# Seven block products in the order 1, 2, 5, 6, 3, 7, 4, with the fifth's copy ahead of the first quarter's rotation on ScalarE

## The chip, the cores and the metric

The kernel runs on one core of a Trainium2 chip. Its engines work beside each other, each through its own queue in order: TensorE (PE for matmuls, PEld for its weight loads), VectorE (DVE), ScalarE (ACT), GpSimd (POOL) and SyncE (SP, which issues most DMAs). The metric is the device time of one execution in microseconds (us), as the median of several runs.

## The reference

The input `x` is 32 sequences of 64 tokens with 512 values each (2048 tokens in all), the context has the same shape. Four residual layers follow each other, all in float32:

```python
x = x + L0_xattn(layernorm(x), ctx)   # 32 query heads, 8 key/value heads of 128, rotary q and k, masked softmax
x = x + L0_ffn(layernorm(x))          # silu(gate) * up, 1376 wide, weights dequantized from 4 bits
x = x + L1_xattn(layernorm(x), ctx)   # the same sizes, q and k normalized by RMS in place of the rotation
x = x + L1_ffn(layernorm(x))          # a memory of 128 slots, top 8, softmax, a gate
```

In an attention layer q = x wq, k = ctx wk, v = ctx wv; scores of the 64 queries of a sequence against its 64 keys, softmax, the weighted sum of v, and that times wo. In the first attention q and k are rotated: `q * cos + rot(q) * sin`, where `rot` exchanges the two halves of a head's 128 rows.

## The kernel before

**Tiles and stages.** The tokens are four chunks of 512 (`NCH`), and an attention layer walks over 32 steps, one for each of eight groups of four heads (`g`) and each chunk (`c`). A step projects k and v (`pk`, L356; `pv`, L388), projects q (tiles `P`, L189), computes scores (`S`, L489), softmax, the values (`po`, L590) and the product with wo (tiles `O`, L189), whose parts are added to x on VectorE (`join`, L237). The work is staggered: in one step, `Attention.run` (L653) emits the rest of the wo products of the step before, then k and q of the next step, then the values of this step, the next step's v, the first wo products, and the next step's scores. The FFN walks over six groups of columns and the four chunks, with up products (tiles `P`, weights `wgu`) and down products (tiles `D`).

**Seven products in place of eight.** The large products (q, wo, up, down) are 512x512 and cut in 2x2 blocks of 256. Each is computed with seven block products of sums of blocks (Strassen's scheme, in Winograd's form). `left_sums` and `right_sums` (L163, L171) make the sums of blocks ahead of time; `PRODUCTS` (L161) says which left and right block each of the seven takes. One block product (`product`, L181) is four float32 matmuls of 128x128 by 128x256; in the trace each shows as two records, so a product is eight records and a call of seven products 56.

**`quarters` (L199)**, which the change edits, is called by `project_q` (L449) and by the FFN's `ffn_up` (L927): 64 calls in the attentions, 24 in the FFN (the last four with half the matmuls). It emits seven products into four PSUM tiles and gives out the four quarters of the result, each as a sum of one copy `h` and one PSUM tile:

- product 1 into tile x; copy 1 of x to `h` on ScalarE (L213); product 2 into a tile of its own: quarter (0,0) is copy 1 plus product 2;
- product 6 added to x; copy 2 of x; product 5 into tile w; copy 5 of w;
- product 3 added to w: quarter (0,1) is copy 2 plus w;
- product 7 added to x; copy 3 of x: quarter (1,1) is copy 5 plus x;
- product 4: quarter (1,0) is copy 3 plus product 4.

So product 6 waits for copy 1, product 7 for copy 2 and product 3 for copy 5: each overwrites by accumulation what the copy reads.

**What `done` does with a quarter.** In the first attention, `quarter` in `project_q` adds on VectorE (L420), then `rotate` (L398) makes two copies of 64 rows on ScalarE (`rq`, L403), two products with cos and sin on VectorE (L405, L406) and a sum on GpSimd into `qT` (L407). In the second attention it is a sum (L438), a square on ScalarE (L440) and a reduction on VectorE (L444). In the FFN it is a sum (L917), silu on ScalarE (L921) for the gate half or a product on GpSimd (L924) for the up half.

**What sets the order.** A scheduler orders each engine's instructions from the order of the program and its own estimates; `tc.issue_after(ins)` adds an edge that queues the block's instructions which run on the engine of `ins` behind it. It adds no wait between engines. In the program that it builds for the kernel before, PE runs products 1, 2, 6, 5, then the first half of 7, then 3, the second half of 7, and 4; ScalarE's queue in the first attention is copy 1, the `rq` pair of the first quarter, copy 2, copy 5, the pair of the second quarter, copy 3, the pairs of the third and fourth.

**Around it.** PSUM holds six tiles of this kind (`mm_tile`, L59), shared by `pk`, `pv`, `P`, `po`, `O`, `D` and the transposes of normalized x (L270). The copies `h` share four buffers (`half_tile`, L68). During the first attention's middle groups the FFN's constants are prepared in pieces on VectorE behind the last `join` of a step (`ffn_constants`, L737, lines L754 to L815); its last group normalizes x for the FFN (`xnb`, L265; `xnT` copies on ScalarE, L274).

Of the kernel before, what the change touches and what calls it, by code (L numbers as in the profile page):

```python
# [44 lines left out]
def tile_xattn_ffn_2_layers(ctx: ExitStack, tc: tile.TileContext, a: dict, out: bass.AP):  # L45
    nc = tc.nc
# [12 lines left out]
    def mm_tile(name):  # L59
        return psp.tile([P, CH], F32, tag="mm", name=name)  # L60
# [7 lines left out]
    def half_tile(name):  # L68
        return ap_.tile([P, CH], F32, tag="half", name=name, bufs=4)
# [111 lines left out]
    def product(which, ps, left, right, widths=(P, P), first=True):  # L181


        nonlocal last_matmul
        l, r = PRODUCTS[which]
        pv = ps.rearrange("p (m n) -> p m n", m=2)
        for m, w in enumerate(widths):
            for k in range(left.shape[2]):
                ins = nc.tensor.matmul(  # L189
                    pv[0:w, m, :],  # L190
                    left[:, l, k, m * P : m * P + w],
                    right[:, r, k, :],
                    start=(first and m == 0 and k == 0),
                    stop=(k == left.shape[2] - 1),
                    skip_group_check=True,
                )
        last_matmul = ins.ins

    def quarters(n, left, right, done, widths=(P, P)):  # L199


        size = (slice(0, widths[0]), slice(0, len(widths) * HC))

        def mul(which, ps=None):
            new = ps is None
            if new:
                ps = mm_tile(f"P{which}_{n}")
            product(which, ps, left, right, widths, first=new)
            return ps

        def copy(which, ps):
            t = half_tile(f"h{which}_{n}")
            nc.scalar.copy(t[size], ps[size])  # L213
            return t

        x = mul(1)
        p1 = copy(1, x)
        done(0, 0, p1, mul(2))
        mul(6, x)
        u2 = copy(2, x)  # L220
        w = mul(5)
        p5 = copy(5, w)
        mul(3, w)
        done(0, 1, u2, w)
        mul(7, x)
        u3 = copy(3, x)
        done(1, 1, p5, x)
        done(1, 0, u3, mul(4))
# [74 lines left out]
    class Attention:  # L303
# [105 lines left out]
        def project_q(self, g, c):  # L409
# [21 lines left out]
            else:  # L431
# [3 lines left out]
                def quarter(i, f, x, y):  # L435
# [11 lines left out]
                    )  # L447

            quarters(n, self.wq[g], xnT[c], quarter)  # L449
            return qT, part  # L450

# [452 lines left out]
    def ffn_up(i, c):  # L904

        if len(ffn_tiles(i)) == 2:
            hT = ctx_tile(f"hT{i}_{c}").rearrange("p a b -> p (a b)")[:, 0 : NBLK * HC]
        else:
            hT = tmp_tile(f"hT{i}_{c}").rearrange("p a b -> p (a b)")
        hT = hT.rearrange("p (b k w) -> p b k w", k=1, w=HC)  # L910
        widths = [w_ for _, w_ in ffn_tiles(i)]
        size = (slice(0, widths[0]), slice(0, len(widths) * HC))

        def quarter(j, half, x, y):

            x, y = x[size], y[size]
            nc.vector.tensor_tensor(x, x, y, ALU.add)  # L917
            h = hT[0 : widths[0], 2 * half : 2 * half + len(widths), 0, :]
            xv = x.rearrange("p (t w) -> p t w", w=HC)
            if j == 0:  # L920
                nc.scalar.activation(xv, xv, AF.Silu)  # L921
                held[half] = xv
            else:
                nc.gpsimd.tensor_tensor(h, held[half], xv, ALU.mult)  # L924

        held = {}
        quarters(f"{i}_{c}", wgu[i], xnT[c], quarter, widths)  # L927
        if len(widths) == 2:
            left_sums(hT)
        return hT  # L930
# [452 lines left out]
```

## Time and profile before

| what | before |
|---|---|
| median of 3 runs | 2912.19 us (2910.71 to 2914.42) |
| the profiled execution | 2913.03 us, of which the span of the profile is 2911.2 |
| TensorE busy | 2824.0 us |
| VectorE, GpSimd, ScalarE busy | 1874.6, 1364.5, 820.0 us |
| q products (tiles `P`, weights `wq`), both attentions | 799.4 us busy, 3584 records |
| up products (tiles `P`, weights `wgu`) | 275.5 us busy, 1232 records |
| copies `h` on ScalarE | 200.3 us, 352 of them |
| `rq` copies on ScalarE | 157.9 us, 256 of them, 617 ns each |
| mean granted TensorE clock | 0.989 |

How to read it: the first attention lies at about 0 to 1210 us, the FFN to 1640, the second attention to about 2870, the last layer's rest behind it. A row of a timeline gives start, duration, engine, line, the operation with output and input tiles and a count, and in brackets the engine's idle time before it with what ended it. A wait row gives total idle time, how often, and the longest. Matmul records overlap: each lasts 379 ns, but the next begins 215 or 216 ns later, so a gap is read from the starts.

### The profile page before, as it was taken

Reading aid. Unit: us, or ns where it says so; the run is one execution under the profiler, and the core shown is the slowest. Engines: PE = TensorE matmul, PEld = TensorE weight load, DVE = VectorE, ACT = ScalarE, POOL = GpSimd, SP = SyncE. Lnnn points to the kernel's source line nnn. Section 1 sums busy time; section 2 is a strip of 40 time slices with the busy share of each in tenths; the row PEclk is TensorE's granted clock in tenths of the full one; section 3 lists DMA queues with packets and bytes.
Section 4 is the critical chain, followed back from the end, with each engine's and each line's share of the span. In section 5 each row is a group of like instructions: output and inputs, shape, how many; then the busy total and the mean of one; then the engine's idle time right before and its main releaser. Section 6 shows DMA issues by size and latency. Waiting matters only on the chain.

```text
span 2911.2 us, 41247 instructions
## 1 busy us (share of the span) xinstructions
PE 2824.0 (97%) x16742; PEld 2262.3 (78%) x16742; DVE 1874.6 (64%) x2809; ACT 820.0 (28%) x1397; POOL 1364.5 (47%) x1038
## 2 busy tenths in 40 slices
PE   7999999999999999899999999999999999999987
PEld 5878787778877887688888677888888888888765
DVE  7677777777777777655555655555555555555567
ACT  3333332333333333111111222222222222222233
POOL 5554545454646454544334444444444444444433
PEclk9999999999999999899999999999999999999998
DMA  4111111111111110100000101111111020201001
GB/s 162 41 41 45 52 46 51 43 52 45 55 53 56 51 45 15 37 22 15 22 14 32 50 30 58 44 51 44 55 40 61 34 66 30 66 30 66 15 1 58
DMA packets 103813, 130.77 MB, mean 45 GB/s; under 512 B 8726, under 2 KB 65166, under 8 KB 103624
## 3 DMA queue, kind: packets, MB, share of 16 engines
q1 hardware_dynamic: 103047, 127.09, 13.2%
q8 instruction: 133, 2.18, 0.3%
q10 hardware_dynamic: 576, 1.05, 0.1%
q14 instruction: 57, 0.46, 0.0%
HBM read 123.92 MB, written 4.19 MB: 44 GB/s over the span
## 4 chain that ended last, share of the span: by engine, by line
PE 85%; DVE 9%; issue 2%; ACT 2%; POOL 1%; DMA 1%; SPq 0%; DVEq 0%; ACTq 0%; POOLq 0%
PE P L189 32%; PE O L189 24%; PE pv L388 8%; PE pk L356 6%; PE po L590 4%; PE S L489 4%; PE D L189 3%; DVE x L237 2%; ACT rq L403 1%; DVE S L512 1%; DVE r2x L549 1%; PE pqy L1077 1%; PE pu L1077 1%; DVE xnd L265 0%; DMA wgu<-in_qweight_gu 0%
## 5 line engine op out<-in xcount | busy, mean ns | idle before, releaser
L189 PE MATMUL P<-xnT,wq 128*128 128x256 f32 x3584 | 799.4, 382 | 22.0 <-ACT h L213 21.7
L189 PE MATMUL O<-wo,oT 128*128 128x256 f32 x3584 | 802.1, 381 | 3.8 <-ACT oT L598 2.4
L189 PEld LDWEIGHTS P<-xnT,wq 128*128 128x128 f32 x3584 | 678.9, 191 | 157.9 <-issue 38.8
L189 PEld LDWEIGHTS O<-wo,oT 128*128 128x128 f32 x3584 | 670.3, 190 | 117.0 <-issue 25.0
L237 DVE TENSOR_TENSOR x<-x,O 128x512 f32<-128x512 f32 (+1 forms) x448 | 368.6, 823 | 228.4 <-PE O L189 228.3
L570 POOL TENSOR_TENSOR s<-s,ib 128x512 f32<-128x512 f32 x128 | 169.4, 1344 | 487.7 <-DVE ib L294 470.5
L407 POOL TENSOR_TENSOR qT<-h,rq 128x512 f32<-128x512 f32 x128 | 175.0, 1367 | 275.7 <-DVE rq L406 266.2
L213 ACT COPY h<-P 128x512 f32<-128x512 f32 (+1 forms) x352 | 200.3, 573 | 354.5 <-PE P L189 351.4
L242 POOL TENSOR_TENSOR qr<-qs,nhalf 128x20 f32<-128x20 f32 x32 | 113.3, 3542 | 358.8 <-DVE qs L477 358.4
L189 PE MATMUL P<-xnT,wgu 128*128 128x256 f32 (+1 forms) x1232 | 275.5, 384 | 2.9 <-DVE x L237 2.7
L564 ACT ACTIVATE s<-s 128x1024 f32<-128x1024 f32 x64 | 67.7, 1057 | 721.6 <-DVE s L562 721.6
L189 PEld LDWEIGHTS P<-xnT,wgu 128*128 128x128 f32 (+1 forms) x1232 | 229.2, 188 | 50.9 <-DVE x L237 11.0
L388 PE MATMUL pv<-wkv,ctxT 128*128 128x128 f32 x1984 | 246.2, 280 | 3.0 <-DVE h L420 1.7
L388 PEld LDWEIGHTS pv<-wkv,ctxT 128*128 128x128 f32 x1984 | 228.5, 192 | 24.3 <-issue 9.9
L403 ACT COPY rq<-h 64x512 f32<-64x512 f32 x256 | 157.9, 617 | 244.5 <-DVE h L420 242.2
L356 PE MATMUL pk<-ctxT,wkv 128*128 128x512 f32 x496 | 223.1, 592 | 0.0
L438 DVE TENSOR_TENSOR qT<-h,P 128x512 f32<-128x512 f32 x128 | 83.9, 674 | 163.8 <-PE P L189 163.8
L356 PEld LDWEIGHTS pk<-ctxT,wkv 128*128 128x128 f32 x496 | 94.1, 190 | 92.9 <-issue 89.6
L405 DVE TENSOR_TENSOR h<-h,cosT 128x512 f32<-128x512 f32 x128 | 90.4, 706 | 104.9 <-ACT rq L403 104.9
L917 DVE TENSOR_TENSOR h<-h,P 128x512 f32<-128x512 f32 (+1 forms) x96 | 59.6, 640 | 141.9 <-PE P L189 112.4
L924 POOL TENSOR_TENSOR hT<-h,h 128x512 f32<-128x512 f32 (+1 forms) x48 | 56.5, 1180 | 200.4 <-DVE h L917 182.7
L598 ACT COPY oT<-po 128x512 f32<-128x512 f32 x256 | 131.5, 601 | 17.7 <-PE po L590 17.0
(248 smaller groups left out, 3433.3 us busy)
## 6 DMA issues: line engine op xcount, KB each, us to landing
ctxT<-in_ctxT SPq DMA_DIRECT2D x62, 1024.0 KB
wq<-in_L_wq SPq DMA_DIRECT2D x32, 256.0 KB
wo<-in_L_wo SPq DMA_DIRECT2D x32, 256.0 KB
wq<-in_L_wqT SPq DMA_DIRECT2D x32, 256.0 KB
wo<-in_L_woT SPq DMA_DIRECT2D x32, 256.0 KB
wgu<-in_qweight_gu SPq DMA_DIRECT2D x40, 128.0 KB
out<-o SPq DMA_DIRECT2D x16, 256.0 KB
x<-in_x SPq DMA_DIRECT2D x12, 256.0 KB
```

What stands on the lines that cost most here:

```text
L189: ins = nc.tensor.matmul(pv[0:w, m, :], left[:, l, k, m * P : m * P + w], right[:, r, k, :], start=(first and m == 0 and k == 0), stop=(k ...
L213: nc.scalar.copy(t[size], ps[size])
L237: return nc.vector.tensor_tensor(dst, dst, src, ALU.add).ins
L242: return nc.gpsimd.tensor_tensor(dst, src, nhalf[:, : src.shape[-1]], ALU.pow).ins
L356: nc.tensor.matmul(ps, wkv[:, k, 0, :], ctxT[:, k, :], start=(k == 0), stop=(k == KT - 1))
L388: nc.tensor.matmul(ps[:, t * HD : (t + 1) * HD], ctxT[:, k, t * P : (t + 1) * P], wkv[:, k, 1, :], start=(k == 0), stop=(k == KT - 1),)
L403: nc.scalar.copy(t[lo:hi, 1], src[HD - hi : HD - lo])
L407: nc.gpsimd.tensor_tensor(dst(None), dst(x), dst(t[:, 1]), ALU.add)
L489: nc.tensor.matmul(s5[j * KB : (j + 1) * KB, f, e], kT[:, f, e, j], qT[:, f * 4 + j].rearrange("p h q -> p (h q)"), start=True, stop=True,)
L570: nc.gpsimd.tensor_tensor(sv[:, f], sv[:, f], ib[:, f * W : (f + 1) * W].unsqueeze(1).to_broadcast([P, KH, W]), ALU.mult,)
L590: nc.tensor.matmul(po[j][:, f * W : (f + 1) * W], v[rows, f, e], probs[rows, f, e], start=(e == 0), stop=(e == KH - 1),)
L598: ins = nc.scalar.copy(o5[:, j], po[j].rearrange("p (x q) -> p x q", q=S))
```

## The change

Inside `quarters`, product 5 and its copy are emitted ahead of products 6, and the first quarter (0,0) is given out behind copy 5, inside `tc.issue_after(last_copy)`, so that the `rq` pair (or the square, or silu) of that quarter is queued on ScalarE behind copy 5. Copy 2 then follows the pair. The seven products, the copies and the sums are the same.

```diff
         def copy(which, ps):
             t = half_tile(f"h{which}_{n}")
-            nc.scalar.copy(t[size], ps[size])
+            nonlocal last_copy
+            last_copy = nc.scalar.copy(t[size], ps[size]).ins
             return t
 
+
+        last_copy = None
         x = mul(1)
         p1 = copy(1, x)
-        done(0, 0, p1, mul(2))
+        y = mul(2)
+        w = mul(5)
+        p5 = copy(5, w)
+        with tc.issue_after(last_copy):
+            done(0, 0, p1, y)
         mul(6, x)
         u2 = copy(2, x)
-        w = mul(5)
-        p5 = copy(5, w)
         mul(3, w)
         done(0, 1, u2, w)
         mul(7, x)
```

Lines below it move down by five: the copies `h` are at L214, the sums L425, the `rq` copies L408, the later lines 5 higher than before.

## Prediction

> **What bounds the kernel now.** I read the page first: which engine is busy, at which clock, and what the chain is made of.
>
> ```profile
> PE 2824.0 (97%) x16742; PEld 2262.3 (78%) x16742; DVE 1874.6 (64%) x2809; ACT 820.0 (28%) x1397; POOL 1364.5 (47%) x1038
> ...
> PEclk9999999999999999899999999999999999999998
> ...
> PE 85%; DVE 9%; issue 2%; ACT 2%; POOL 1%; DMA 1%; SPq 0%; DVEq 0%; ACTq 0%; POOLq 0%
> ```
>
> TensorE is the bound nearly everywhere, so a change pays only by the TensorE gaps that it closes. Second, the waits of PE and of its weight loads (total us, times, longest):
>
> ```profile
> PE P L189 <- ACT h L213: 21.7, 14, 3.8
> ```
>
> ```profile
> PEld P L189 <- ACT h L213: 36.3, 69, 4.2
> ```
>
> The P products wait for ScalarE's copies `h`: 14 open gaps, and 69 late weight loads, most of them hidden. Third, the timeline of one attention call with a gap, then of one without:
>
> ```profile
> 600.80 7.07 PE L189 MATMUL P<-xnT,wq 128*128 128x256 f32 x32
> ...
> 602.73 0.59 ACT L213 COPY h<-P 128x512 f32<-128x512 f32 x1 [0.50 <-PE P L189]
> 602.90 1.88 DVE L793 CAST szoh<-zi 4x344 bf16<-4x344 uint32 x1
> ...
> 606.01 0.68 DVE L420 TENSOR_TENSOR h<-h,P 128x512 f32<-128x512 f32 x1
> ...
> 606.78 1.25 ACT L403 COPY rq<-h 64x512 f32<-64x512 f32 x2 [3.47 <-DVE h L420]
> 608.05 1.07 ACT L213 COPY h<-P 128x512 f32<-128x512 f32 x2
> ...
> 608.78 5.42 PE L189 MATMUL P<-xnT,wq 128*128 128x256 f32 x24 [0.91 <-ACT h L213]
> ```
>
> ```profile
> 708.24 12.33 PE L189 MATMUL P<-xnT,wq 128*128 128x256 f32 x56
> ...
> 712.75 1.24 ACT L403 COPY rq<-h 64x512 f32<-64x512 f32 x2 [1.99 <-DVE h L420]
> 714.01 0.58 ACT L213 COPY h<-P 128x512 f32<-128x512 f32 x1
> ...
> 715.35 0.59 ACT L213 COPY h<-P 128x512 f32<-128x512 f32 x1 [0.75 <-PE P L189]
> ...
> 715.99 4.18 PEld L189 LDWEIGHTS P<-xnT,wq 128*128 128x128 f32 x20 [0.21 <-ACT h L213]
> ```
>
> A call is 56 records, eight per product, 215.5 ns apart: 1.72 us per product. At 600.80, 32 records (products 1, 2, 6, 5) run; then product 7 (its first half stands ahead of 3) waits for copy 2, which stands behind the rotation's two `rq` copies, which wait for VectorE's sum L420, held up by the FFN's constants (L793). At 708.24 the sum is on time; there only the weight load for product 3 waits, 0.21 us, for copy 5, and the matmul starts show a step of 295 ns in place of 216.
>
> So I took from the trace's start times, call by call, the length from first to last record beyond 55 steps (11.865 us). First attention: 33.8 us in 32 calls. FFN: 6.0 in 24. Second attention: 9.1 in 32.
>
> **The change, part by part.** Times are from a call's first matmul.
>
> *Product 5 third, copy 5 second.* The built order (each engine's instructions as the scheduler leaves them) has it so in every call: PE runs 1, 2, 5, 6, 3, 7, 4 and no longer splits product 7 around 3, so that the change does what it says is settled. Copy 1 starts at 1.93 (710.17 in the second call), so copy 5, 3.45 later in PE's order, runs 5.38 to 5.96. Its readers: product 3 starts at 6.90 (32 steps), 0.9 late enough. Product 6 needs copy 1 alone. Product 5 needs its PSUM bank 1.72 earlier; in the rows of before the bank's last reader ends 2.6 us or more before it (2.6 in one short FFN call, where the move is 0.86; 3.6 elsewhere). Cost 0; without that cover at most 1.72 a call.
>
> *The rotation behind copy 5.* This is the added wait: on ScalarE the `rq` pair, copy 2, the second pair and copy 3 queue behind copy 5. The pair, which began at 4.51, begins at 5.99; with 1.25 for it and 0.61 for copy 2 (606.78 to 608.64), copy 2 ends at 7.85. Product 7 now starts after 40 steps, at 8.62, and a copy needs 0.14 to release it (608.64 to 608.78): spare 0.63. Hence product 7 stalls only where the pair starts after 6.62, that is where L420 ends after 6.53. The call at 600.80 (L420 ends at 5.9) loses its whole stall. No instruction or DMA is added but 49 semaphore instructions of 17 ns on an idle ScalarE; SP's order is unchanged.
>
> *Downstream.* The next rows have little spare: O's product 1 begins a median 0.37 us after its oT copy, pv 0.41 after L420's last. But the second quarter's sum, which ran at 9.85 (718.09), now needs product 3 at 8.8 and copy 2, so it runs at 8.9; pairs two to four and the oT copies follow 0.9 earlier. So the spare grows, and what PE gains it keeps.
>
> Sum, first attention (excess over 11.865):
> - 11 calls stalled by 0.3 to 1.4 us: 6.9, and 14 with only late weight loads: 1.6. All go: 8.5.
> - Calls at 194.70, 343.36, 488.80: 5.6 + 2.1 + 4.8 = 12.5. The pair started there at 8.82, 6.95, 7.99, so 2.20, 0.33, 1.37 stay, with 0.1 of late loads each: gain 8.2.
> - Calls at 1099.63 and 1140.00: 2.1 + 3.0. In the built order the `xnT` copies now stand behind the third and fourth pair, and a po product needs their PSUM bank: by the same chaining the second xnT copy ends at 17.1 instead of 15.9, and pv starts where it did. Gain 0.3.
> - Start: the call at 39.89 keeps its stall (ScalarE's exp still stands ahead of copy 2), but VectorE's built order puts the last sums ahead of two normalisations, for which pv waited 1.7 (63.35). I take 1.0; bounds -0.5 and 1.7.
>
> FFN: 20 calls lose 0.106 each, 2.2 (the rest is VectorE's joins). Second attention: 9.1 less 6.0 of the call at 1668.50, where exp stands ahead of the late copy before and after: 3.1.
>
> 8.5 + 8.2 + 0.3 + 1.0 + 2.2 + 3.1 = 23.3 us. The profiled execution took 2913.03 (span 2911.2, 1.8 around it), the median of three is 2912.19: 2889.7 and 2888.9. I say **2889**.
>
> Of the 8.2, 3.1 is clock: after the stalls of 3.82 and 2.99 us about eight matmuls ran at twice the step; none did after 2.88 or 2.01.
>
> ```profile
> 206.00:208.00 2.00, 2.00 (x7) 0.58 0.00 0
> ```
>
> The column 0.58 is the granted clock just after the first. The stalls left over (2.20, 1.37) are below both, so I take it all back. The Trainium skill ("TensorE: Matmul & The Clock Gate", "Part 1: The HAM clock gate") puts the return to half clock after an idle window of about 3.4 us; the trace agrees for 3.82 and differs for 2.99. By that rule alone the second call's 1.7 us would not hang on its stall, and the sum would be 21.6.
>
> **The rivals.**
> - *Late loads only move.* Product 7 has 0.63 spare, but loads were late at spares of up to 0.07 in the rows; if 0.63 does not cover them either, 1.6 + 2.2 + 3.1 are not gained: 2896. Against: calls with 0.44 to 0.6 spare at record 32 (708.24 is one) show no step there.
> - *Given back at O and pv.* If the later rows keep their place in time (the rotation is bound by VectorE and POOL, not by PE), each first-attention call keeps at most 0.37: 14 small ones 1.6, 14 others 5.0, and 5.3 from the other stages: 2901. Against: in the call at 708.24 each later pair waits for a sum that waits for PE (718.09, idle 2.78 for PE).
> - *Not slower, but the same:* VectorE's sum was the cause and is not moved; if it slips by as much as the slack gained (its order with POOL changes): 2910.
> - *Slower: product 7 becomes the stall.* The pair begins 1.5 us later everywhere. If the sum L420 were held with it (it is not in the built order, where only ScalarE's instructions follow copy 5), or the pair and copy 2 took 0.63 longer, all 32 first-attention calls stall. It decides at a copy 2 ending at 8.48; at 9.6, 1.1 us a call, 35 us are lost against 23 gained: 2924. The Trainium skill (same page, the table of specifications) calls ScalarE's queue strictly first in, first out, so the pair can't pass a late copy 5; the trace agrees (608.05: two copies back to back behind the pair).
>
> **How the numbers follow.** Forecast 0.62 (alone 2884 to 2894); late loads 0.12; given back 0.14; the same 0.07; slower 0.05. The range leaves out the last two: from the full recovery of the left-over stalls (2881) to given back (2902). A measurement tells 0.2% (5.8 us) from no change, so faster is the first three less a bit, 0.86; same 0.08; slower 0.06.
>
> **What would show it.** Right: PE's waits of P for h fall from 21.7 to about 10, in six or seven places; PEld's from 36.3 to under 15; most attention calls take 56 records in 12.2 us without a gap; O's wait for oT does not grow; the `rq` pair begins 6.0 after a call's start. Wrong: a gap at record 40 in the calls without VectorE's extra work, a larger "O <- oT" or "pv <- h", or steps of 295 ns at records 33 or 41.

## The result, and the profile after

The changed kernel takes 2894.39 us in the median of six runs (2890.91 to 2897.4), the kernel before on the same chip 2913.8 (2910.71 to 2917.59): a ratio of 0.9931, with a 95% interval of 0.9921 to 0.9941. The profiled execution took 2894.59 us, 18.4 less than that of before; 23.3 were forecast (2889, range 2881 to 2902).

The page of the changed kernel, engines and chain:

```profile
PE 2816.7 (97%) x16742; PEld 2270.3 (78%) x16742; DVE 1892.6 (65%) x2809; ACT 824.6 (29%) x1397; POOL 1345.6 (47%) x1038
...
PE 88%; DVE 6%; POOL 1%; ACT 1%; issue 1%; DMA 1%; SPq 0%; DVEq 0%; ACTq 0%; POOLq 0%
```

VectorE has gone from 9% to 6% of the chain, ScalarE from 2% to 1%. The waits of PE (total us, times, longest), then that of its weight loads:

```profile
PE P L189 <- ACT h L214: 9.7, 5, 3.8
...
PE po L595 <- ACT xnT L279: 2.5, 2, 1.3
PE O L189 <- ACT oT L603: 2.4, 2, 1.2
...
PE pv L393 <- DVE h L425: 1.6, 4, 0.6
```

```profile
PEld P L189 <- ACT h L214: 11.1, 7, 4.2
```

The wait for `h` fell from 21.7 to 9.7 and from 36.3 to 11.1 for the loads; O's wait for oT is what it was. The wait of po for `xnT`, 2.5 us, is new (before, pv waited 1.3 us for it). The call that stood at 600.80 with a gap of 0.91 us:

```profile
590.82 12.25 PE L189 MATMUL P<-xnT,wq 128*128 128x256 f32 x56
...
596.20 0.58 ACT L214 COPY h<-P 128x512 f32<-128x512 f32 x1 [2.87 <-PE P L189]
596.52 0.68 DVE L425 TENSOR_TENSOR h<-h,P 128x512 f32<-128x512 f32 x1
...
597.29 1.24 ACT L408 COPY rq<-h 64x512 f32<-64x512 f32 x2 [0.51 <-DVE h L425]
598.56 0.58 ACT L214 COPY h<-P 128x512 f32<-128x512 f32 x1
```

The sum ends 6.4 us into the call, later than before (5.9), and the pair follows it. But copy 5 is already done (596.20 to 596.78), copy 2 ends at 599.14, 8.3 us into the call, and product 7 is due only at 8.6: all 56 records run without a step longer than 216 ns. This holds for 24 of the 32 first-attention calls, now 11.87 us long.

The time by stage, from the start times of the calls' first matmuls (us; the excess is call length beyond 11.865, summed):

| stretch | before | changed | gain |
|---|---|---|---|
| to the third call | 86.56 | 87.90 | -1.3 |
| third call to the last but one | 1013.07 | 999.78 | 13.3 |
| from there to the FFN's first call | 114.46 | 115.34 | -0.9 |
| FFN | 429.46 | 424.69 | 4.8 |
| second attention to its last call | 1137.06 | 1132.37 | 4.7 |
| the rest of the span | 130.58 | 132.72 | -2.1 |
| excess, first attention | 33.8 | 13.5 | 20.4 |

The last row is the important one: the q calls of the first attention alone became 20.4 us shorter, yet the first attention (the first three rows) only 11.1.

### The profile page after: what moved, and what is told of

Read it like the earlier page. It is cut to its first block, busy times and chain, and to the rows that moved or that the text cites. A ratio compares the mean times of both kernels' runs of the same rounds, so it can differ in the third digit from the quotient of the medians.

```text
span 2892.8 us, 41295 instructions
## 1 busy us (share of the span) xinstructions
PE 2816.7 (97%) x16742; PEld 2270.3 (78%) x16742; DVE 1892.6 (65%) x2809; ACT 824.6 (29%) x1397; POOL 1345.6 (47%) x1038
## 4 chain that ended last, share of the span: by engine, by line
PE 88%; DVE 6%; POOL 1%; ACT 1%; issue 1%; DMA 1%; SPq 0%; DVEq 0%; ACTq 0%; POOLq 0%
PE P L189 33%; PE O L189 26%; PE pv L393 8%; PE pk L361 7%; PE S L494 4%; PE po L595 4%; PE D L189 3%; DVE x L242 1%; ACT rq L408 1%; PE pqy L1082 1%; PE pu L1082 1%; DVE h L425 0%; DVE h L410 0%; PE pd L962 0%; DVE xnd L270 0%
## 5 line engine op out<-in xcount | busy, mean ns | idle before, releaser
L189 PE MATMUL P<-xnT,wq 128*128 128x256 f32 x3584 | 787.8, 380 | 10.0 <-ACT h L214 9.7
L214 ACT COPY h<-P 128x512 f32<-128x512 f32 (+1 forms) x352 | 202.4, 575 | 567.5 <-PE P L189 557.0
L408 ACT COPY rq<-h 64x512 f32<-64x512 f32 x256 | 157.9, 617 | 124.8 <-DVE h L425 119.8
L449 DVE TRANSPOSE_TENSOR_REDUCE part<-q 128x16 f32<-128x512 f32 x128 | 90.6, 709 | 91.6 <-ACT q L445 87.7
```

Source lines behind the costliest of these rows:

```text
L189: ins = nc.tensor.matmul(pv[0:w, m, :], left[:, l, k, m * P : m * P + w], right[:, r, k, :], start=(first and m == 0 and k == 0), stop=(k ...
L214: last_copy = nc.scalar.copy(t[size], ps[size]).ins
L408: nc.scalar.copy(t[lo:hi, 1], src[HD - hi : HD - lo])
```

## The experiments

**Theory:** what pays is that copy 5 is queued ahead of the rotation pair *and* that product 7 comes a product later, so that the copy behind the pair is wanted 1.72 us later. **Rivals:** the product order alone, or the place in the queue alone, gives the gain; VectorE's lateness is not the cause; and, for the missing 5 us, that the gains are given back at po, pv and O.

| kernel | median us | before, same chip | ratio (95%) |
|---|---|---|---|
| order alone | 2914.95 | 2915.32 | 1.0001 (0.9992 to 1.0011) |
| queue alone | 2911.22 | 2915.32 | 0.9988 (0.9979 to 0.9997) |
| first attention alone | 2899.98 | 2915.72 | 0.9947 (0.9928 to 0.9965) |
| copy 2 three times | 2913.76 | 2915.32 | 0.9997 (0.9987 to 1.0006) |
| VectorE's pieces moved (on before) | 2956.33 | 2915.32 | 1.0139 (1.0124 to 1.0154) |
| both copies ahead | 2937.86 | 2915.72 | 1.0076 (1.0057 to 1.0096) |
| both ahead in five calls | 2892.96 | 2915.72 | 0.9922 (0.9906 to 0.9938) |
| norm later | 2885.84 | 2915.72 | 0.9899 (0.9883 to 0.9915) |
| norm later, on before | 2910.35 | 2913.77 | 0.9987 (0.9978 to 0.9997) |

**The product order alone.**

```diff
-        with tc.issue_after(last_copy):
-            done(0, 0, p1, y)
+        done(0, 0, p1, y)
```

> The seven products in the new order, but the first quarter's rotation is not held: its two rq copies stand ahead of copy 5 on ScalarE, as they stood ahead of copy 2 before. Theory (what pays is that nothing that TensorE needs at record 32 stands behind the rotation pair): copy 5 is now behind the pair and product 3 needs it at record 32, 6.90 us into the call, the same date as product 7's in the kernel before. The stalls stay and move from product 7 to product 3: PE's wait of P for h stays near 21 us (20 to 23), gaps at record 32 in place of 40. Only the late weight loads of the second copy can go (copy 2 is now wanted 1.7 us later): 2 to 6 us. Time 2908 to 2912. Rival (the product order alone gives product 7 its 1.7 us and that is all it takes): wait of P for h about 10 us, time 2893 to 2898.

It gains nothing: 2914.95 us lies above the 2908 to 2912 expected. The wait for `h` did not stay at 20 to 23 us but grew from 21.7 to 26.6, and the call that had a gap of 0.91 us shows where it went:

```profile
605.93 7.07 PE L189 MATMUL P<-xnT,wq 128*128 128x256 f32 x32
...
611.60 0.68 DVE L424 TENSOR_TENSOR h<-h,P 128x512 f32<-128x512 f32 x1
...
612.37 1.24 ACT L407 COPY rq<-h 64x512 f32<-64x512 f32 x2 [3.93 <-DVE h L424]
613.63 1.07 ACT L214 COPY h<-P 128x512 f32<-128x512 f32 x2
...
614.36 5.42 PE L189 MATMUL P<-xnT,wq 128*128 128x256 f32 x24 [1.37 <-ACT h L214]
```

Again 32 records, then a gap: now product 3 waits for copy 5, which stands behind the pair. The excess of the first attention rose from 33.8 to 41.3 us. In the FFN and the second attention, however, this kernel has nearly the whole gain: 0.13 us in most of the 20 full FFN calls and 0.08 or 0.14 in those of the attention, as in the changed kernel. So the rival fails where the rotation is, and holds where there is none: there the hold does nothing. At 613.63 both copies, ready before, start when the pair ends: ScalarE's queue is served in order here. The Trainium skill says so too ("TensorE: Matmul & The Clock Gate", table of specifications: strictly first in, first out).

**The queue alone:** the order of products before, the rotation held behind copy 2.

```diff
-        done(0, 0, p1, mul(2))
+        y = mul(2)
         mul(6, x)
         u2 = copy(2, x)
+        with tc.issue_after(last_copy):
+            done(0, 0, p1, y)
```

> The product order of the kernel before (1, 2, 6, 5, half of 7, 3, rest of 7, 4), but the first quarter's rotation is held behind copy 2 on ScalarE. Theory: copy 2 runs at 5.4 to 6.0 us and product 7's first half at record 32 is never late; copy 5 is now the one behind the pair, and product 3 wants it at record 36, 7.76 us in, 0.86 us later than copy 2 was wanted. The pair starts at 6.0 or later, so copy 5 ends at 7.85 or later and product 3 is late by 0.2 us in every one of the 32 first-attention calls, and by 0.86 less than before where VectorE's sum is late. PE's wait of P for h 12 to 18 us with gaps at record 36; first attention gains 4 to 8 us in all, time 2903 to 2910. Rival (the place of the pair in ScalarE's queue is all that counts): wait about 10, time 2893 to 2898.

The gaps are where the theory put them, at record 36, and of the size it gave: 0.13 to 0.22 us and a late load of 0.1 in every clean call, and 0.86 us less than before in the late calls (those at 194.70, 343.36, 451.99, 600.80 and 1099.63 before). In the call at 711.25:

```profile
717.24 1.24 ACT L407 COPY rq<-h 64x512 f32<-64x512 f32 x2
718.51 0.59 ACT L214 COPY h<-P 128x512 f32<-128x512 f32 x1
...
719.14 4.18 PEld L189 LDWEIGHTS P<-xnT,wq 128*128 128x128 f32 x20 [0.36 <-ACT h L214]
```

The pair now waits for nothing, but copy 5 behind it ends at 719.10, 7.85 us into the call, and product 3 was due at 7.76. The time missed the expected 2903 to 2910 by one: between the third call and the last but one only 1.7 us are gained, since the call at 491.34 is 1.6 us longer in place of 0.9 shorter (its stall grew from 2.99 to 3.33 us, and thirteen records behind it took twice the step in place of eight), and from the first call to the third this kernel takes 4.6 us more. In the first attention, the two halves of the change need each other.

**The change in the first attention alone** (`if n.count("_") == 2 and n[0] == "0":` the new order with the hold, `else:` the old emission).

> The change in the first attention alone; FFN and second attention keep the order of products and the queue of the kernel before. Theory after the run of the product order alone (there the FFN and second-attention calls lost their 0.13 and 0.08 us each without the hold): the first attention gains what it gains in the changed kernel, 10 to 12 us at the first FFN call, and nothing after it but the one call at 1362 whose clock fell (1.8 us, which may or may not fall here): 6 us more than the changed kernel, 2899 to 2903. Rival (all the gain is in the first attention): 2894 to 2896.

As expected: from the third call to the last but one it takes 999.77 us (changed kernel 999.78), every stall and give-back is repeated within 0.03 us, and the FFN and second-attention calls keep their 0.13 and 0.08 to 0.14 us.

**Copy 2 done three times**, with product 4 held behind product 7:

```diff
         u2 = copy(2, x)
+        if n.count("_") == 2 and n[0] == "0":
+            for _ in range(2):
+                nc.scalar.copy(u2[size], x[size])
...
+        with tc.issue_after(last_matmul):
+            z = mul(4)
```

> The changed kernel with copy 2 done three times over in the 32 first-attention calls (the same data into the same tile), and product 4 held behind product 7 so that the order of the products stays. Tests the spare of 0.63 us at record 40 and the slower rival. Theory: the pair ends at 7.24, three copies of 0.53 to 0.61 us end at 8.9 to 9.1, product 7 starts 0.14 after that, 9.0 to 9.2 in place of 8.62: a gap of 0.4 to 0.6 us in each of the 32 calls, and 1.1 us more in the five that still stall: 13 to 19 us more than the changed kernel, 2907 to 2914, PE's wait of P for h 23 to 30 us. Other view (the later pairs and the oT copies take the delay, 1.1 us a call, and O or pv wait as well): more than 25 us, over 2919. If the spare were more than 1.1 us: 2895.

```profile
PE P L189 <- ACT h L230: 23.4, 32, 3.5
```

All 32 calls have a gap at record 40; the clean ones are 0.60 us longer, 0.5 of gap and 0.1 of late load, and the distance between calls grew by those 0.60, no more. This prices the rival "product 7 becomes the stall" and places its start: with 0.63 us spare, 1.1 us more on ScalarE costs 0.5.

**VectorE's lateness.** On the kernel before, the pieces of the FFN's constants are emitted behind project_q:

```diff
-                    with tc.issue_after(self.added):
-                        for hook in late.get((g, c), ()):
-                            hook()
...
                     qT, part = self.project_q(*steps[i + 1])
+                    for hook in late.get((g, c), ()):
+                        hook()
```

> The kernel before, with the FFN-constant pieces of VectorE put behind project_q in program order instead of ahead of project_k, so that the sum L420 is not held up by them. Theory (the stalls come from VectorE being late with the first quarter's sum): 14 stalls of 19.4 us in the first attention, 3.1 of it clock, nearly all go, also with the old order; the late weight loads (1.6 there, 2.2 in the FFN, 3.1 in the second attention) stay. PE's wait of P for h falls from 21.7 to about 5, time 2894 to 2900, if the pieces find room later in the call; if they push the second quarter's sums, pv or po wait for a part of it, up to 8 us. Rival (the pieces are not the cause, the pair is late anyway): 2908 to 2913.

```profile
PE O L189 <- DVE x L237: 29.0, 18, 4.7
PE P L189 <- ACT h L213: 15.7, 4, 7.4
```

As to the cause the theory holds: 27 of the 32 calls have no gap at record 32 and are 11.95 or 12.01 us long, with the old order. As to the price it fell: the kernel is 41 us slower. In the call at 507.02 pieces still ran ahead of the sum, which came at 518.84: that is the wait of 7.4 us. Behind project_q the pieces stand ahead of the joins `x` of the wo products that VectorE does next, and O waited 29.0 us for joins in 18 places (before, 0.5 in one). From the third call to the last but one it takes 1052.2 us in place of 1013.1; how the rest of that came about was not traced. So with the pieces in either place VectorE is late for something; the change leaves it late and moves what depends on it.

**Both copies ahead of the rotation**, in every call:

```diff
-        with tc.issue_after(last_copy):
-            done(0, 0, p1, y)
         mul(6, x)
         u2 = copy(2, x)
+        with tc.issue_after(last_copy):
+            done(0, 0, p1, y)
```

> The changed kernel with the first quarter's rotation held behind both copies, 5 and 2, in every call. Theory (the pair has little room behind it): all stalls at product 7 that come from the pair go (5.5 us in the first attention; the two start calls stay, where exp stands ahead of copy 2). But the pair starts at 7.7 in place of 6.0, the second at 11.2 in place of 9.7 behind copy 3, the fourth and the four oT copies end about 0.9 us later, and O's product 1, which starts 0.27 us after the last oT copy in a call of the changed kernel, waits about 0.6 us in most of the 32 calls: O's wait for oT rises from 2.4 to 15 to 20 us, time 2902 to 2912. Rival (the pairs and oT copies have room, so the earlier a copy for a product the better): 2888 to 2891.

```profile
PE O L189 <- ACT oT L603: 42.1, 31, 3.0
...
PE P L189 <- ACT h L214: 3.8, 1, 3.8
```

The excess of the first attention is 0.2 us: no stall at all, and the kernel is 22 us slower than before. In a clean call:

```profile
689.82 12.25 PE L189 MATMUL P<-xnT,wq 128*128 128x256 f32 x56
...
700.99 2.52 ACT L408 COPY rq<-h 64x512 f32<-64x512 f32 x4
...
705.82 0.68 DVE L425 TENSOR_TENSOR h<-h,P 128x512 f32<-128x512 f32 x1
...
706.59 1.24 ACT L408 COPY rq<-h 64x512 f32<-64x512 f32 x2 [3.08 <-DVE h L425]
...
707.85 2.05 ACT L603 COPY oT<-po 128x512 f32<-128x512 f32 x4
...
708.98 3.84 PE L189 MATMUL O<-wo,oT 128*128 128x256 f32 x16 [1.21 <-ACT oT L603]
```

The direction was expected, the size not (0.6 us a call expected, 1.6 measured), and the cause is another one. The third pair (the second half of the row at 700.99) is not late: it begins 12.4 us into the call, in a clean call of the changed kernel 12.9. But the scheduler also put the last quarter's sum on VectorE behind the third rotation (705.82), the fourth pair waits 3.08 us for it, and the oT copies start 18.0 us into the call in place of 15.5. So this run does not show that the pair can't wait for two copies; with that sum in its old place it was not run.

**Both copies ahead in five calls alone** (`if n in ("0_1_1", "0_2_1", "0_3_1", "0_7_2", "0_7_3"):`, the hold behind copy 2, else behind copy 5).

> The changed kernel, with the rotation held behind copy 2 as well in five calls alone, those at 195.74, 339.81, 482.75, 1087.68 and 1131.30, where VectorE's sum is late anyway. Theory: in these the pair starts at 7.3 to 9.2 whatever stands before it, copy 2 is ready at 7.7, so the stalls of 2.45, 0.59, 1.84, 0.30 and 0.28 us go and the pairs are not later: 4 to 5.5 us if the rest of the call follows PE, 2889 to 2891. Rival (the rotation is bound by VectorE in these calls, so that O and po wait for the oT copies and for s by what PE gains): 2893 to 2896.

```profile
PE O L189 <- ACT oT L609: 9.0, 5, 2.3
PE P L189 <- ACT h L214: 5.4, 2, 3.8
```

For the first three calls the rival has the outcome right: they became 2.56, 0.69 and 1.94 us shorter, and the next call came 0.30, 1.16 and 3.08 us *later* against the changed kernel. In time, then, nothing is won there. That the rotation was bound by VectorE is not shown, though: in these five calls too the last sum stands behind the third rotation, and in the call at 194.30 the third pair begins 2.0 us earlier than in the changed kernel, the fourth 1.1 us later. What this kernel gains it gains at the end: 110.2 us in place of 115.3 from the last call but one to the FFN, where the `xnT` copies again stand ahead of the fourth pair. That leads to the next.

**Norm later.** In the first attention, `norm_apply` for the FFN is emitted behind po and the oT copies:

```diff
-                if done:
+                if done and self.L == 1:
                     after(before[1])
                 oT = self.values(g, c, v, probs)
+                if done and self.L == 0:
+                    after(before[1])
```

> The changed kernel with the normalisation behind the first attention's last group (norm_apply, its transposes and xnT copies) emitted behind po and the oT copies in place of ahead of po. It tests the loss after the call at 1087.68, where po waited 1.26 us for an xnT copy and pv then took 6.51 in place of 3.84 us. Theory (the xnT copies stand ahead of what po and pv need): those 4 us come back and the FFN starts 3 to 5 us earlier, time 2889 to 2892. Rival (the copies only move the wait on to pv's v copy, to O or to the FFN): 2893 to 2897.

First the place in the changed kernel: four `rq` copies, the four `xnT` copies behind them, po waiting for a PSUM bank that they read, and pv at half clock; then the clock at the end of po and the start of pv (the column before the last two; from 1104.4 to 1106 it was 1.00):

```profile
1101.22 2.52 ACT L408 COPY rq<-h 64x512 f32<-64x512 f32 x4 [1.40 <-DVE h L425]
...
1103.76 2.05 ACT L279 COPY xnT<-xtb 128x512 f32<-128x512 f32 x4
...
1104.40 3.04 PE L595 MATMUL po<-s,v 32*128 32x256 f32 x26 [1.26 <-ACT xnT L279]
...
1107.37 6.51 PE L393 MATMUL pv<-wkv,ctxT 128*128 128x128 f32 x32
```

```profile
1106.00:1108.00 2.00, 2.00 (x15) 1.24 (x9) 0.14 (x1) 1.36 (x3) 1.72 (x2) 0.54 0.00 0
```

And the same place with the norm later:

```profile
1099.74 2.01 PE L595 MATMUL po<-s,v 32*128 32x256 f32 x32
...
1103.88 1.14 PE L275 MATMUL xtb<-ident,xnb 128*128 128x128 f32 x8 [1.11 <-ACT oT L603]
...
1104.86 3.84 PE L393 MATMUL pv<-wkv,ctxT 128*128 128x128 f32 x32
```

The stretch takes 106.8 us in place of 115.3, the kernel 2885.84 us (2884.96 to 2888.28, all below the changed kernel's runs): the fastest version here. It gained more than the 3 to 5 us expected, since the last po now runs where PE waited for VectorE's normalised x (4.3 us of `xtb` waits for `xnb`, now gone; `xtb` waits 2.2 us for the oT copies in their place).

**The same edit on the kernel before.**

> The kernel before, with norm_apply emitted behind po and the oT copies as in the fastest version. It tells whether the 8 us that this gave the changed kernel are a loss that the change had brought in, or an older one. Theory (half and half): in the kernel before two xnT copies stood ahead of the third pair and no po waited for them, so the call at 1099.63 keeps its place and only the stalls and xtb waits of the last two first-attention calls change: 2 to 5 us, 2909 to 2912. Rival (the loss is older than the change and all of it can be had without it): 2905 to 2908. If it was all the change's own: 2912 to 2917.

The stretch takes 113.5 us in place of 114.5, or 2.6 less if one leaves out that the clock fell once more in it (1.7 us, in the call at 1141.98). So of the 8.6 us that the edit gives the changed kernel there, some 6 to 7.6 (8.6 less 2.6 or 0.9) are a loss that the change had brought in, and the rest is older. Of the 8.6, 3.4 are the half clock of po and pv at 1106 to 1114. Without what half clock took, the edit gives 5.1 us there and 2.6 in the kernel before, and the difference is po's two waits, 2.5. That the wait of po brought the fall of the clock is not shown: an equal wait at 1148.00 had none behind it.

## Why the prediction was right, and where its sum was off

The mechanism is as predicted, and both its conditions are shown: order alone and queue alone give 0 and 0.1%. The change does what it says, the pair waits behind copy 5, and no gap arises at record 40 in calls without VectorE's extra work. By the terms of the sum:

- **Ordinary calls, 8.5.** Right: all gaps and late loads of these calls are gone but 0.07 us in the first and 0.12 at 447.25. "Late loads only move" is refuted by 24 calls without one longer step.
- **The three long stalls, 8.2.** Measured 7.3. The stalls left are 2.45, 0.59 and 1.84 us in place of 2.20, 0.33 and 1.37. The step that failed is that the pair keeps its place in the call: it started at 9.18, 7.31 and 8.56 us in place of 8.82, 6.95 and 7.99. VectorE's sum slipped by 0.36, 0.36 and 0.57: a small part of the rival "the same". The slip is there from the call's start: a piece ahead of the sum, the same one in both kernels, begins at 1.11, 1.68 and 1.34 us in place of 0.75, 1.32 and 0.77. Why it does so stays open.
- **The clock, 3.1 of it.** All of it came back: no half-speed steps followed the 2.45 and 1.84. That was also luck: in other kernels they followed stalls of 2.05 to 2.34 us. My own bound between 2.88 and 2.99 us does not order these runs (see the last section). Nor does the Trainium skill's idle window of about 3.4 us ("TensorE: Matmul & The Clock Gate", "Part 1: The HAM clock gate").
- **Downstream, nothing given back.** This failed, in the middle and at the end. In the middle the calls gained 15.5 us and the stretch 13.3: the waits of pv for L425 and late loads of the following po and O products took 2.2 us, in four steps; the rival "given back" has so much of the truth. At the end the two last calls became 4.3 us shorter, and the stretch, where 0.3 of gain was forecast, 0.9 us longer: 5.2 lost. I had seen the `xnT` copies behind the pairs and reckoned that pv "starts where it did". In sum it does: with po waiting 1.26 us in both calls, pv starts 0.58 us later in the one and 0.88 earlier in the other. What I had put at nothing is what came behind: pv took 6.51 in place of 3.84 us once, 2.7 lost at half clock. The norm-later kernel gives this back.
- **Start, 1.0.** Measured -1.3, nearly all of it ahead of the first call, where the change edits nothing: that call begins at 22.45 us before and 23.73 here. It begins at 23.85 in the norm-later kernel on before, which does not differ from before there, and at 22.93 to 23.73 in the four (this one, first attention alone, norm later, both ahead in five calls) that do not differ from each other there. From the first call to the third, 0.1 us is lost in place of the 1.0: pv's wait did fall, from 1.7 to 0.6, but `pk` now waits 0.9 us for L425.
- **FFN, 2.2.** Measured 4.8: 2.5 of it in the calls (0.13 in place of 0.106 each), and 1.8 from one call in the kernel before, at 1362.86, in which the clock had fallen. With the old order in the FFN it does not fall there either (first attention alone: 427.46 us), so the new order is not what spares it.
- **Second attention, 3.1.** 0.08 or 0.14 us a call, 2.8 us as the order-alone kernel has it; the changed kernel's 4.7 holds 1.2 from the stretch ahead of the last call. That stretch, and the rest of the span (130.3 to 133.4 us in eleven profiles), differ by 2 to 3 us between kernels that do not differ there.

Against the forecast, then, the middle lacks 3.4 us, the start 2.3, the rest of the span 2.1 and the end 1.2, some 9 in all; FFN and second attention hold 4.2 more than forecast, of which 1.8 and 1.2 are not shown to be the change's. So it is in part luck that the sum was only 5 us too high. The steps that failed are the place of the late pairs, the give-backs in the middle, and the end, where the wait was seen but not the clock behind it; the range, which reached to "given back", held the result.

## What to carry to other kernels

Where an in-order queue serves both a slow chain and a copy that the bound engine needs, look at each operation's due date in the bound engine: reorder the products so that the copy that must stand behind the chain is wanted latest, and put just the one that is wanted first ahead of it. With both copies ahead the stall vanished here, but another engine's queue came out in another order as well, and that cost more: look at every queue that an edit leaves behind. After a change, ask at which point in the queues the *next* stage's work now stands; the loss at 1104 us was there, and moving the norm gave 8.6 us in that stretch, as much as the change's largest term.

## What the runs showed of the hardware that was not expected

The granted clock does not follow the length of a stall. By the matmuls' start times, some seven to fourteen records took twice the step after stalls of 2.05, 2.28, 2.30, 2.34, 2.95 and 2.99 us, and none did after 2.01, 2.45, 3.01 and 3.36. After 2.88 us, in the last q call of the first attention, they did in one kernel (VectorE's pieces moved, 1182.10) and not in another (before, 1140.00). In the same call of the same order, 2.99 us was followed by it (before, 488.80) and 3.01 was not (norm later on before, 491.15). After 3.36 us in the order-alone kernel the clock (third column from the right) stood at full speed:

```profile
507.00:511.00 4.00, 4.00 (x35) 3.31 (x37) 2.63 (x5) 2.08 (x4) 0.81 (x1) 1.00 0.02 4
```

At 1104.40 it fell after an idle time of 1.26 us, and only some 1.6 us after PE had started again; after a wait of 1.27 us at 1148.00 it did not. The Trainium skill ("TensorE: Matmul & The Clock Gate", "Part 1: The HAM clock gate") says that the window is free-running, which would let equal stalls end differently; but a whole idle window of 3.4 us does not fit into 2.05 to 2.99 us, and here the measurement decides. What sets it was not found. For a forecast it means 1.7 to 3 us of uncertainty for each stall of 2 to 3.4 us.
